# Batch 1 of a cross attention gets the form of batches 2 to 5: two output products in seven blocks, a joint state of y, one subtraction by transfer

## The chip, the cores and the metric

The kernel runs on one core of a Trainium2 chip. The metric is the device time of one execution in microseconds; of several executions the median counts. A core has TensorE (PE, matmuls into PSUM; PEld is its loading of weights), VectorE (DVE), ScalarE (ACT), GpSimd (POOL) and SyncE (SP). Each works through its own queue in order, and the queues meet by semaphores. SP and POOL also start transfers; a transfer that adds to what its destination holds goes out from POOL.

## The reference

Eight batches; x1 and x2 are 512 x 1024 (channels x positions) each, the weights map to 64 channels for queries and keys and to 512 for values, all in float32:

```
q = einsum('bcn,dc->bnd', x1, Wq) + bq
k = einsum('bcn,dc->bdn', x2, Wk) + bk
v = einsum('bcn,dc->bdn', x2, Wv) + bv
attn = softmax(einsum('bnd,bdm->bnm', q, k), axis=2)
out = einsum('bcm,bnm->bcn', v, attn) + x1
```

## The kernel before

The values are never formed. With E the exponentials of the scores (positions of x2 by positions of x1), the kernel computes y = x2 E, scales its columns by one over the sums of E, and then the result Wv y + bv + x1. Both products, y and the result ("o" in names), are 512-row products that are split in 2 x 2 blocks and done in seven block products in place of eight (numbered 1 to 7, `MULT`), with sums of the operands' blocks formed by VectorE beforehand: T1 to T4 of the right operand, S1 to S4 of the left. A block product may be split the same way once more: "in seven blocks" means seven matmul groups of 256 columns in place of plain ones of 512. Its small sums come from `left_stream` and `right_stream` (or `inner_right`), its matmuls from `inner_product` (line 635), or in `multiply_41` from line 1023. Each float32 matmul leaves two records in the trace.

Within a seven-block product the accumulators are shared out with copies on ScalarE: a "chain" in a PSUM bank of its own takes block 1, is copied to one half of a bank, takes block 6, is copied to the next, takes block 5, and so on, so that block 6 can start only when block 1 has been copied. Block 7 (the "third") is copied out to v and added by VectorE at the end: that add is what the calls `complete_7()`, `complete_3()` and so on issue (line 915, in `multiply_41` line 999).

`period(s, n, nn, nnn)` is one batch's stage. It holds the second half of batch s (scaling, products of the result) woven with the first half of batch n, the next one: its scores, the maxima over them (`fold`, `fold_halves`, `highest`), the subtraction of the maximum (`lower`, line 343, 128 x 1024 elements each), and its exponentials. In order, for batch 1: products 1, 2 and 6 of y; scores of the next batch's first half; queries; products 5, 7 and 3 of y; scores of the second half; keys; product 4 of y woven with product 1 of the result (`multiply_41`); products 6, 2, 5, 7, 3 and 4 of the result. Nothing is planned at run time: the schedule is manual, and each engine's queue holds its instructions in the order in which these calls issue them. Hooks (`{6: ...}`) put a ScalarE instruction behind a given block of a product.

Flags of a batch pick between variants. `six` (batches 2 to 6): product 6 of y in seven blocks and y's blocks joined by transfers. `three` (batches 2 to 5): products 3 and 6 of the result in seven blocks, through `ORDER41_3`, which appends product 6 of the result to `multiply_41`, and `multiply_all_573` (5, 7 and 3 together). Batches 0, 1 and 6 do product 6 by `second(6)` (line 521: four plain matmuls of 512 columns) and 5, 7 and 3 by `multiply_57`, where product 3 is plain (line 834).

What the prediction's steps touch:
- `copy_7` (line 1061): ScalarE takes the two halves of product 7 of y, negated, into `tmp[7]`. Half 1 needs `complete_7()`.
- `join_67` (line 1051): VectorE adds `tmp[7]` to `tmp[6]`; `evict_y(s, "22")` (line 1089): VectorE adds that to the accumulator of products 1, 6 and 5 and so forms block 22 of y. In batches 2 to 6 ScalarE copies the accumulator instead (`copy_22`, line 358), and two accumulating transfers add the rest.
- `evict_t3` (line 1066), `scale_y` (line 1073), `sum_y` (lines 478 and 480): blocks of y and their sums.
- `evict_y(s, "21")` and `scale_y(s, "21")`: block 21, which product 2 of the result reads.
- `turn_top` and `lower_late`: the maximum negated on ScalarE, and one of the four subtractions as an accumulating transfer.
- `join_o6`, `copy_o6`: the accumulators of the result's products 1 and 6 joined, and copied out.
- `evict_o`: the result's blocks with bias; block 12 goes through ScalarE without a third summand, or through VectorE with product 3 as one.

Of the kernel before, what the change touches and what calls it, by code (L numbers as in the profile page):

```python
# [11 lines left out]
ALU = mybir.AluOpType  # L12
# [3 lines left out]
def kernel(  # L16
# [47 lines left out]
    nc = tc.nc  # L64
    P = 128
    B, C, N = x1.shape
# [57 lines left out]
    class Batch:  # L124
        def __init__(self, b):
            self.b = b
            self.a, self.e, self.t, self.y, self.o = {}, {}, {}, {}, {}
            self.mx, self.top, self.den, self.few, self.rden, self.row = {}, {}, {}, {}, {}, {}
            self.tmp, self.bank = {}, {}
            self.inner = {}  # L130
            self.six = 2 <= b < B - 1
            self.three = 2 <= b < B - 2
            self.lent = b == B - 2 and not self.six
            self.one = b >= 1

# [19 lines left out]
    def copied_s4(s):  # L155

        s.a["S4"] = sb.tile([P, MH, C // 2], F32, tag="aS4", name=f"aS4_{s.b}")
        nc.scalar.mul(s.a["S4"], s.a["S2"], -1.0)
# [195 lines left out]
    def copy_22(s, j):  # L354

        if j == 0:
            s.y["22"] = sb.tile([P, 2, H], F32, tag="y22", name=f"y22_{s.b}")
        nc.scalar.copy(s.y["22"][:, j, :], s.bank["a", j])
# [45 lines left out]
    def begin_t1(s, i):  # L404
        nc.scalar.mul(s.t["T1"][:, i : i + 2, :], s.t["22"][:, i : i + 2, :], -1.0)
# [147 lines left out]
    def weave(*streams):  # L553

        streams = list(streams)
        while streams:
            for stream in list(streams):
                if next(stream, "end") == "end":
                    streams.remove(stream)
# [32 lines left out]
    def right_stream(s, i, x, *tags):  # L592

        half = x.shape[1] // 2
        v = {f"{q + 1}{r + 1}": x[:, ts(q, half), ts(r, H // 2)] for q in range(2) for r in range(2)}
        last = 4 // len(tags)
        shape = [P, last, half, H // 2]
        sums = [
            sb.tile(shape, F32, tag=t, name=f"eI{i}{t}_{s.b}") if isinstance(t, str) else t for t in tags
        ]  # L600
        if i in (1, 2):
            for z, k in enumerate(("T1", "T2", "T4", "T3")):
                v[k] = sums[z // last][:, z % last]
            s.inner[i, "t"], s.inner[i, "m"] = v, sums[-1][:, last - 2 : last]
            sums_t = (
                ("T1", "12", "11", ALU.subtract),
                ("T3", "22", "12", ALU.add),
                ("T2", "T3", "11", ALU.subtract),
                ("T4", "21", "T2", ALU.subtract),
            )  # L610
            for k, x, y, op in sums_t if i == 1 else sums_t[1:3] + sums_t[:1] + sums_t[3:]:
                nc.vector.tensor_tensor(v[k], v[x], v[y], op)
                yield
            return
        both, t2, t4 = sums[0][:, 0:2], sums[-1][:, last - 2], sums[-1][:, last - 1]
        part = x.rearrange("p (q k) (r n) -> p q k r n", q=2, r=2)
        nc.vector.tensor_tensor(
            both, part[:, :, :, 1, :], part[:, 0].rearrange("p k r n -> p r k n"), ALU.subtract
        )
        s.inner[i, "t"] = v | {"T1": both[:, 0], "T3": both[:, 1], "T2": t2, "T4": t4}  # L620
        yield
        nc.vector.tensor_tensor(t2, both[:, 0], v["22"], ALU.subtract)
        yield
        nc.vector.tensor_tensor(t4, v["21"], t2, ALU.add)
        yield
# [424 lines left out]
    def join_67(s):  # L1050
        nc.vector.tensor_tensor(s.tmp[6], s.tmp[6], s.tmp[7], ALU.add)
# [6 lines left out]
    def copy_7(s, j):  # L1058
        if j == 0:
            s.tmp[7] = sb.tile([P, 2, H], F32, tag="u1", name=f"uy7_{s.b}")  # L1060
        nc.scalar.mul(s.tmp[7][:, j, :], s.bank["c", j], -1.0)
# [253 lines left out]
    def period(s, n, nn, nnn):  # L1315
# [138 lines left out]
            scale_y(s, "11", "T3", "22")  # L1454
        else:
            complete_1 = multiply_seeded(s, 1, "y11", {
                4: lambda: copied_s4(s), 6: lambda: begin_t1(s, 2) if (s.six or s.lent) and s.b > 2 else None
            } if s.b > 1 else {2: lambda: exponential(s, 1, 3)})
            early = s.b > 1 and n is not None
            def second_product():  # L1460
# [94 lines left out]
                for leave in s.leave:  # L1555
                    leave()
            if n:
                sums_3 = right_stream(s, 3, s.t["22"], "eT2" if s.six else "eT1")
                if s.six:
                    if nn is None:  # L1560
                        complete_7()
                    weave(left_stream(s, 3, s.a["S4"], "a12"))
                    if s.b > 1:
                        spread(s, 1)
                    else:
                        shares(s, 1)
                    if nn:
                        complete_7()
                    weave(sums_3)
                else:  # L1570
                    next(sums_3)
                    if s.b == 1:
                        shares(s, 1)
                    weave(*([left_stream(s, 3, s.a["S4"], "aI3")] if nn else []), sums_3)
                if nn or not s.six:
                    lower(n, 0, 0)
            else:
                inner_right(s, 3, s.t["22"], "eT1")
            hooks = {}
            if s.six:  # L1580
                if nn:
                    lower(n, 0, 1)
                complete_5 = multiply_seeded(s, 5, "yT4", {7: lambda: copy_7(s, 0), 6: lambda: copy_7(s, 1)}, "a")
                nc.gpsimd.dma_start(s.tmp[6], s.tmp[7], accum_op=ALU.add)
                complete_5()
                if nn is None:
                    lower(n, 0, 0)
                    lower(n, 0, 1)
                hooks |= {1: lambda: copy_22(s, 0), 7: lambda: copy_22(s, 1)}
            else:  # L1590
                complete_7 = multiply_seeded(
                    s, 7, "y12", {} if n else {6: lambda: copy_22(s, 0), 4: lambda: copy_22(s, 1)}
                )
                complete_7()
                if n is None:
                    shares(s, 1)
                    inner_left(s, 4, s.a["22"], "a12")
                    scale_y(s, "11")
                    inner_right(s, "o1", s.y["11"], "i2")
                copy_7(s, 0)  # L1600
                if n:
                    hooks[7] = lambda: copy_7(s, 1)
                else:
                    copy_7(s, 1)
                    nc.gpsimd.dma_start(s.tmp[6], s.tmp[7], accum_op=ALU.add)
                    nc.gpsimd.dma_start(s.y["22"], s.tmp[6], accum_op=ALU.add)
            if n:
                hooks |= {6: lambda: exponential(n, 0, 0), 4: lambda: exponential(n, 0, 1)}
            if n and not s.six:
                lower(n, 0, 1)  # L1610
            complete_3 = multiply_seeded(s, 3, "r", hooks, "c")
            if s.six:
                if nn:
                    lower(n, 0, 2)
                turn_top(n)
                nc.gpsimd.dma_start(s.y["22"], s.tmp[6], accum_op=ALU.add)
                lower_late(n)
            if n is None:
                right_4 = right_stream(s, 4, s.t["T4"], "eT2")
                next(right_4)  # L1620
            if n and not s.six:
                join_67(s)
                evict_y(s, "22")
            if n is None:
                weave(right_4)
            if n:
                weave(left_stream(s, 4, s.a["22"], "aI3" if s.six else "a12"), right_stream(s, 4, s.t["T4"], "eT1" if s.six else "eT2"))
            if s.six and nn is None:
                complete_3()
                evict_t3(s)  # L1630
            if s.six and s.b > 1:
                scale_y(s, "11")
                inner_right(s, "o1", s.y["11"], "i2")
            if not s.six or nn:
                complete_3()
                evict_t3(s)
        if n:
# [96 lines left out]
        if five:  # L1734
            if nn is None:
                scale_y(s, "22")
            elif not s.three:
                next(sums_o7)
            if s.three:
                products = multiply_all_573(s, while_573)  # L1740
                next(products)
                join_o6(s)
                copy_o6(s)
            sum_y(s, "T1")
            if nn is None:
                next(sums_o7)
                fold(n, 1, 3, "max", ALU.max)
                highest(n, 1)
                weave(sums_o7)
                lower(n, 0, 2, ALU.add)  # L1750
            weave(
                in_turn(lowers(n, 0, MH if s.six else 2, MH), lowers(n, 1, 0, 2)),
                iter(()) if s.three else sums_o7,
            )
        if s.b == 0:
# [16 lines left out]
            second(6)  # L1772
        if s.b == 0:
            exponential(n, 0, 3)
        if five and not s.six:
            exponential(n, 0, 2)
        if s.b == 0:
            negate(n, "S3")
        elif n:
# [146 lines left out]
```

## Time and profile before

| | us |
|---|---|
| median of three runs (lowest, highest) | 660.95 (660.47, 661.91) |
| the profiled execution's own time | 659.96 |
| its span, first to last instruction | 658.2 |
| from batch 1's next scores to batch 2's | 80.34 |
| the same of batches 2, 3, 4, 5 | 79.53, 79.52, 79.70, 79.53 |

In the profile's rows a time is in microseconds from the span's start; a row of a timeline gives start, duration, engine, line, operation, what is written and read, the shape and how many instructions were merged, and in brackets the idle time ahead of it and what ended it. A row of the windows gives the stretch, its length, and each engine's busy time (with the number of its instructions), then TensorE's granted clock, the DMA engines' busy share and what they moved. A TensorE record's end is modelled, so its pace is read from starts. Times of ScalarE, VectorE and TensorE can overlap slightly from one instruction to the next, since they are pipelined.

### The profile page before, as it was taken

What the parts mean: (1) busy time and instruction counts of PE and PEld (TensorE: products, weight loads), DVE (VectorE), ACT (ScalarE), POOL (GpSimd) and SP (SyncE); (2) the same over time, 40 slices, a digit from 0 to 9 for tenths busy, and PEclk for the clock granted to TensorE, in tenths of its full rate; (3) what the DMA queues carried; (4) which work ended last, traced back from release to release, by engine and by line L of the source; (5) the groups of instructions that cost most, each with busy time, mean ns of one, the idle gap of its engine ahead of it and who ended that gap; (6) DMA issues with size and microseconds to landing.
All of it is one profiled execution on the core that took longest, in us unless ns stands there. A gap on an engine that the chain in (4) does not pass through costs nothing.

```text
span 658.2 us, 8303 instructions
## 1 busy us (share of the span) xinstructions
PE 653.7 (99%) x2686; PEld 445.1 (68%) x2686; DVE 623.2 (95%) x907; ACT 409.1 (62%) x804; POOL 233.0 (35%) x208
## 2 busy tenths in 40 slices
PE   9999999999999999999999999999999999999997
PEld 4435755757658667687677786776866777666865
DVE  1999999999899999999999999999999999999996
ACT  3855457446485577865777657776577757575432
POOL 0125215622237322383233822347213553145410
PEclk9999999999999999999999999999999999999999
DMA  9869578994789979999999999999997899789834
GB/s 328 296 218 295 114 252 149 214 259 148 237 177 222 243 232 297 211 199 225 264 308 207 199 253 234 311 209 194 272 262 154 193 195 266 178 161 203 159 81 149
DMA packets 52186, 144.27 MB, mean 219 GB/s; under 512 B 5936, under 2 KB 6448, under 8 KB 52144
## 3 DMA queue, kind: packets, MB, share of 16 engines
q0 software_dynamic: 25152, 70.33, 57.3%
q1 hardware_dynamic: 26848, 73.29, 31.3%
q8 instruction: 21, 0.34, 0.2%
q14 instruction: 21, 0.17, 0.1%
q10 hardware_dynamic: 144, 0.14, 0.1%
HBM read 87.83 MB, written 16.81 MB: 159 GB/s over the span
## 4 chain that ended last, share of the span: by engine, by line
PE 99%; DVE 0%; issue 0%
PE ps_yc L635 9%; PE ps_ya L635 8%; PE ps_oc L521 7%; PE ps_s L238 7%; PE ps_q L193 4%; PE ps_i7chain L635 3%; PE ps_i4b L1023 3%; PE ps_k L193 3%; PE ps_i5chain L635 3%; PE ps_ya L521 3%; PE ps_i3chain L635 3%; PE ps_oa L834 3%; PE ps_oc L1023 3%; PE ps_i1chain L635 3%; PE ps_i2chain L635 3%; PE ps_i4chain L1023 3%
## 5 line engine op out<-in xcount | busy, mean ns | idle before, releaser
L367 ACT ACTIVATE e<-e 128x1024 f32<-128x1024 f32 x60 | 62.9, 1060 | 14.8 <-DVE e L343 14.5
L343 DVE TENSOR_TENSOR e<-e,top 128x1024 f32<-128x1024 f32 x55 | 65.9, 1224 | 0.2 <-POOL top L275 0.2
L275 POOL PARTITION_ALL_REDUCE top<-max x16 | 30.1, 1884 | 81.6 <-DVE max L269 62.4
L247 ACT COPY e<-ps_s 128x512 f32<-128x512 f32 x92 | 48.9, 620 | 11.6 <-PE ps_s L238 9.5
L238 PE MATMUL ps_s<-q,k 64*128 64x512 f32 (+1 forms) x192 | 47.5, 598 | 0.0
L307 POOL PARTITION_ALL_REDUCE den<-sum x10 | 32.6, 3259 | 29.4 <-DVE sum L269 24.5
L259 DVE TENSOR_TENSOR max<-max,e 128x1024 f32<-128x1024 f32 x29 | 35.3, 1218 | 0.6
L238 PEld LDWEIGHTS ps_s<-q,k 64*128 64x128 f32 x192 | 17.9, 186 | 19.9 <-issue 16.0
L1073 DVE TENSOR_TENSOR y<-y,den 128x1024 f32<-128x1024 f32 x24 | 29.2, 1221 | 0.3
L898 ACT COPY ps_yc<-ps_i7chain 128x256 f32<-128x256 f32 x32 | 11.5, 361 | 26.5 <-PE ps_i7chain L635 13.0
L288 POOL PARTITION_ALL_REDUCE den<-sum x6 | 19.4, 3232 | 21.4 <-DVE sum L269 21.4
L193 PE MATMUL ps_q<-x_in_x_dram,wqk_sb 128*64 128x512 f32 x112 | 25.6, 598 | 0.0
L521 PE MATMUL ps_oc<-yT,w 128*128 128x512 f32 x56 | 25.2, 592 | 0.0
L381 DVE TENSOR_TENSOR eT<-e,e 128x1024 f32<-128x1024 f32 (+1 forms) x18 | 24.5, 1384 | 0.1
L898 ACT COPY ps_ya<-ps_i5chain 128x256 f32<-128x256 f32 x32 | 11.4, 357 | 21.2 <-PE ps_i5chain L635 17.0
L586 DVE TENSOR_TENSOR aI<-a 128x256 f32<-128x256 f32 x58 | 23.9, 411 | 0.0
L635 PE MATMUL ps_yc<-e,aI 128*128 128x256 f32 x92 | 23.7, 380 | 0.0
L898 ACT COPY ps_yc<-ps_i3chain 128x256 f32<-128x256 f32 x32 | 11.5, 359 | 16.9 <-PE ps_i3chain L635 12.8
L193 PE MATMUL ps_k<-x_in_x_dram,wqk_sb 128*64 128x512 f32 x96 | 21.9, 598 | 0.0
L328 POOL DMA_DIRECT2D den<-row x12 | 6.7, 555 | 42.9 <-DMA row<-few 37.8
L521 PE MATMUL ps_oc<-y,w 128*128 128x512 f32 x48 | 21.6, 592 | 0.0
L171 POOL DMA_DIRECT2D aS<-in_x2T_dram x7 | 9.8, 1407 | 32.9 <-ACT aS L167 32.9
(431 smaller groups left out, 1961.5 us busy)
## 6 DMA issues: line engine op xcount, KB each, us to landing
x_in_x_dram<-in_x_dram SPq DMA_DIRECT2D x60, 512.0 KB, 9.1
a<-in_x2T_dram SPq DMA_DIRECT2D x32, 512.0 KB, 10.5
eT<-eT POOLq DMA_DIRECT2D x26, 512.0 KB, 8.0
aS<-in_x2T_dram POOLq DMA_DIRECT2D x22, 512.0 KB, 9.1
uo<-in_x_dram POOLq DMA_DIRECT2D x18, 512.0 KB, 11.2
e<-e POOLq DMA_DIRECT2D x14, 512.0 KB, 7.3
out_dram<-uo SPq DMA_DIRECT2D x11, 512.0 KB, 11.9
r<-in_x_dram POOLq DMA_DIRECT2D x10, 512.0 KB, 8.1
```

Of the source, the lines that this page charges most:

```text
L193: nc.tensor.matmul(ps[r, :], w_sb[:, c, :], s.x[:, c, ts(h, H)], start=(c == 0), stop=(c == CT - 1),)
L238: nc.tensor.matmul(ps[g][:, n], s.k[r, ts(i, P)], s.q[r, ts(h, H)][:, n], start=True, stop=True)
L247: nc.scalar.copy(e[:, g, i, :], ps[g])
L259: nc.vector.tensor_tensor(f, e[:, :, 0, :] if i == 1 else f, e[:, :, i, :], op)
L275: nc.gpsimd.partition_all_reduce(s.top[h], s.mx[h][:, 0, :], P, ReduceOp.max)
L307: nc.gpsimd.partition_all_reduce(s.den[h], s.mx[h][:, 0, :], P, ReduceOp.add)
L343: nc.vector.tensor_tensor(e, e, top, op)
L367: nc.scalar.activation(e, e, AF.Exp)
L521: nc.tensor.matmul(ps, left[ka][:, k, ts(j, P)], right[kb][:, k, :], start=opens and k == 0, stop=i in (2, 3, 4) and k == n_k - 1, skip_gr ...
L635: nc.tensor.matmul(ps, s.inner[i][ka][:, k, :], s.inner[i, "t"][kb][:, k, :], start=opens and k == 0, stop=z in (2, 3, 4) and k == n_k - 1 ...
L898: nc.scalar.copy(out, of)
L1023: nc.tensor.matmul(ps, s.inner[i][ka][:, k, :], s.inner[i, "t"][kb][:, k, :], start=opens and k == 0, stop=z in (2, 3, 4) and k == n_k - 1 ...
```

## The change

`three` holds for batch 1 too, so that its result takes the way of batches 2 to 5: product 6 of the result follows product 1 within `multiply_41`, products 5, 7 and 3 come from `multiply_all_573`, block 12 of the result is finished by VectorE, and batch 2's T1 is begun behind a block of its product 1. Beside that, within batch 1: block 22 of y is copied from the accumulator by ScalarE behind blocks 6 and 4 of product 7, both halves of product 7 are copied right behind product 7, and two accumulating transfers form block 22, in place of `join_67` and `evict_y`; of batch 2's four subtractions of the maximum for its first half the third moves ahead of product 4 and the fourth becomes a transfer (`lower_late`); the scaling of block 11 and its sums for product 1 of the result move ahead of `complete_3()`; the third fold of batch 2's second maximum, which batch 1 had left out, is done; the sums for product 3 of y and for product 4 swap their buffers (eT1, eT2).

```
-            self.three = 2 <= b < B - 2
+            self.three = 1 <= b < B - 2
...
-                4: lambda: copied_s4(s), 6: lambda: begin_t1(s, 2) if (s.six or s.lent) and s.b > 2 else None
+                4: lambda: copied_s4(s), 6: lambda: begin_t1(s, 2) if (s.six or s.lent) and s.b > 1 else None
...
-                sums_3 = right_stream(s, 3, s.t["22"], "eT2" if s.six else "eT1")
+                sums_3 = right_stream(s, 3, s.t["22"], "eT2" if s.one and n else "eT1")
...
                 complete_7 = multiply_seeded(
-                    s, 7, "y12", {} if n else {6: lambda: copy_22(s, 0), 4: lambda: copy_22(s, 1)}
+                    s, 7, "y12", {6: lambda: copy_22(s, 0), 4: lambda: copy_22(s, 1)}
                 )
                 complete_7()
...
                 copy_7(s, 0)
-                if n:
-                    hooks[7] = lambda: copy_7(s, 1)
-                else:
-                    copy_7(s, 1)
-                    nc.gpsimd.dma_start(s.tmp[6], s.tmp[7], accum_op=ALU.add)
-                    nc.gpsimd.dma_start(s.y["22"], s.tmp[6], accum_op=ALU.add)
+                copy_7(s, 1)
+                nc.gpsimd.dma_start(s.tmp[6], s.tmp[7], accum_op=ALU.add)
+                nc.gpsimd.dma_start(s.y["22"], s.tmp[6], accum_op=ALU.add)
...
             complete_3 = multiply_seeded(s, 3, "r", hooks, "c")
-            if s.six:
+            if n:
                 if nn:
                     lower(n, 0, 2)
                 turn_top(n)
-                nc.gpsimd.dma_start(s.y["22"], s.tmp[6], accum_op=ALU.add)
+                if s.six:
+                    nc.gpsimd.dma_start(s.y["22"], s.tmp[6], accum_op=ALU.add)
                 lower_late(n)
...
-            if n and not s.six:
-                join_67(s)
-                evict_y(s, "22")
...
-                weave(left_stream(s, 4, s.a["22"], "aI3" if s.six else "a12"), right_stream(s, 4, s.t["T4"], "eT1" if s.six else "eT2"))
+                weave(left_stream(s, 4, s.a["22"], "aI3" if s.six else "a12"), right_stream(s, 4, s.t["T4"], "eT1"))
...
-            if s.six and s.b > 1:
+            if n:
                 scale_y(s, "11")
                 inner_right(s, "o1", s.y["11"], "i2")
-            if not s.six or nn:
+            if n is None or nn:
                 complete_3()
                 evict_t3(s)
...
-                in_turn(lowers(n, 0, MH if s.six else 2, MH), lowers(n, 1, 0, 2)),
+                in_turn(lowers(n, 0, MH, MH), lowers(n, 1, 0, 2)),
                 iter(()) if s.three else sums_o7,
...
-        if five and not s.six:
-            exponential(n, 0, 2)
```

## The prediction

> **What bounds the kernel now.** I read the page first (busy times, then the chain that ended last), then the windows between the first score matmuls of one batch and the next, then each engine's timeline around batch 1 and the same stretch of batch 2, which already has the form that batch 1 is to get.
>
> ```profile
> PE 653.7 (99%) x2686; PEld 445.1 (68%) x2686; DVE 623.2 (95%) x907; ACT 409.1 (62%) x804; POOL 233.0 (35%) x208
> PEclk9999999999999999999999999999999999999999
> PE 99%; DVE 0%; issue 0%
> ```
>
> The chain that ended last is TensorE and nothing else, at the full granted clock. A busy PE row need not mean that its array is always fed, so I look at its pace: the starts of its groups.
>
> ```profile
> core 0: us, PE busy (x) PEld busy (x) DVE busy (x) ACT busy (x) POOL busy (x), PEclk, DMA share, GB/s
> 133.71:214.05 80.34, 80.34 (x330) 55.08 (x329) 77.98 (x115) 50.17 (x96) 29.37 (x24) 1.00 0.84 210
> 155.00:165.00 10.00, 10.00 (x47) 5.70 (x47) 9.96 (x16) 8.56 (x16) 0.54 (x1) 1.00 0.10 30
> 214.05:293.58 79.53, 79.53 (x343) 57.39 (x342) 76.64 (x114) 55.57 (x112) 30.93 (x29) 1.00 0.98 238
> ```
>
> ```profile
> 153.11 1.03 PE L635 MATMUL ps_i3chain<-e,aS 128*128 128x256 f32 x4
> 153.97 1.03 PE L635 MATMUL ps_i3third<-eI3eT,aI 128*128 128x256 f32 x4
> 154.84 1.03 PE L635 MATMUL ps_i3chain<-eI3eT,aI 128*128 128x256 f32 x4
> ...
> 159.25 1.99 PE L238 MATMUL ps_s<-q,k 64*128 64x512 f32 x8
> ...
> 166.47 1.13 PE L1023 MATMUL ps_i4chain<-eT,a 128*128 128x256 f32 x4
> ...
> 175.64 3.60 PE L521 MATMUL ps_oa<-yT,w_S 128*128 128x512 f32 x8
> 179.07 3.60 PE L521 MATMUL ps_oc<-y,w 128*128 128x512 f32 x8
> ...
> 195.82 1.03 PE L635 MATMUL ps_i1chain<-e,a 128*128 128x256 f32 x4
> ```
>
> ```profile
> 246.81 1.13 PE L1023 MATMUL ps_i4chain<-eT,a 128*128 128x256 f32 x4
> ...
> 259.87 3.60 PE L521 MATMUL ps_oc<-y,w 128*128 128x512 f32 x8
> ...
> 275.35 1.03 PE L635 MATMUL ps_i1chain<-e,a 128*128 128x256 f32 x4
> ```
>
> Groups of four 256-column records start 0.86 us apart (153.11, 153.97, 154.84), the eight 512-column records of a plain output product take 3.43 us (175.64 to 179.07), and no gap stands between groups. So TensorE is paced by its own work in both batches: what takes matmul time away shortens the run, and each stall that is added lengthens it for good, since no idle stretch follows in which to catch up. VectorE is the next to bind: 77.98 of the 80.34 us from batch 1's scores to batch 2's, and 76.64 of the following 79.53.
>
> **The change part by part.** *TensorE's saving.* Products 3 and 6 of the result go from 8 records of 512 columns to 14 of 256 each: 14 x 0.86/4 = 3.02 us in place of 3.43, 0.41 each, 0.82 in all. The two batches say the same: from product 4 of y to the next batch's first product, batch 1 takes 195.82 - 166.47 = 29.35 us and batch 2 275.35 - 246.81 = 28.54. Saving: 0.81 us.
>
> *ScalarE's order.* Block 22 of y now comes from the accumulator by two copies while product 7 runs, and both copies of product 7 stand ahead of product 3, where the second stood behind product 3's second block.
>
> ```profile
> 153.31 0.60 ACT L1061 ACTIVATE uy<-ps_yc 128x512 f32<-128x512 f32 x1 [0.51 <-PE ps_yc L635]
> 154.23 0.36 ACT L898 COPY ps_yc<-ps_i3chain 128x256 f32<-128x256 f32 x1 [0.32 <-PE ps_i3chain L635]
> ...
> 155.31 0.60 ACT L1061 ACTIVATE uy<-ps_yc 128x512 f32<-128x512 f32 x1
> ```
>
> ```profile
> 149.10 1.69 DVE L617 TENSOR_TENSOR eI3eT<-e 128x1024 f32<-128x1024 f32 x1
> ...
> 154.46 0.69 DVE L915 TENSOR_TENSOR ps_yc<-ps_yc,v 128x512 f32<-128x512 f32 x1
> 155.06 1.21 DVE L343 TENSOR_TENSOR e<-e,top 128x1024 f32<-128x1024 f32 x1
> 156.19 1.21 DVE L1051 TENSOR_TENSOR uy<-uy,uy 128x1024 f32<-128x1024 f32 x1
> 157.44 1.29 DVE L1089 TENSOR_TENSOR y<-ps_ya,uy 128x512 f32<-128x512 f32 x2
> 158.65 0.41 DVE L586 TENSOR_TENSOR aI<-a 128x256 f32<-128x256 f32 x1
> ...
> 162.32 0.69 DVE L915 TENSOR_TENSOR ps_yc<-ps_yc,v 128x512 f32<-128x512 f32 x1
> ...
> 173.20 0.70 DVE L999 TENSOR_TENSOR ps_oc<-ps_oc,v 128x512 f32<-128x512 f32 x1 [0.79 <-ACT ps_oc L1032]
> ...
> 175.48 0.70 DVE L999 TENSOR_TENSOR ps_i4b<-ps_i4b,v 128x512 f32<-128x512 f32 x1 [0.99 <-ACT ps_i4b L1032]
> ...
> 177.53 1.23 DVE L1073 TENSOR_TENSOR y<-y,den 128x1024 f32<-128x1024 f32 x1
> ```
>
> The second copy of product 7 reads what VectorE's add at 154.46 leaves at 155.15; nothing ahead of that add moves in VectorE's queue. Handing over costs 0.09 us (product 3's first group ends at 153.11 + 1.03, ScalarE starts at 154.23). So that copy runs from 155.24 to 155.84, and behind it in ScalarE's queue waits the copy of product 3's chain (0.36), which stood at 154.23 and now ends at 156.2. TensorE's third block of product 3 adds to that chain and must wait for it: 156.3 in place of 154.84, a stall of 1.4 us. Its bounds: 0 if the add came before 153.9, 1.4 as the rows stand. The two copies of block 22 (0.6 each, the copy at 153.31 being as large) fall into the waits that ScalarE has during product 7 and cost nothing.
>
> *VectorE ahead of product 4.* The sum of products 6 and 7 and the two sums into block 22 (156.19 to 158.65, 2.46 us) go. In their place comes the third subtraction of the maximum (1.13, as from 155.06 to 156.19), so the sums for product 4 begin at 157.32. They take 3.67 (158.65 to 162.32) and end at 160.99. Then, ahead of the add that completes product 3, come the scaling of block 11 and the sums for the result's product 1, which stood behind it. Batch 2 has that order:
>
> ```profile
> 238.60 1.22 DVE L1073 TENSOR_TENSOR y<-y,den 128x1024 f32<-128x1024 f32 x1
> ...
> 241.39 0.69 DVE L915 TENSOR_TENSOR ps_yc<-ps_yc,v 128x512 f32<-128x512 f32 x1
> ...
> 252.22 1.22 DVE L1073 TENSOR_TENSOR y<-y,den 128x1024 f32<-128x1024 f32 x1
> 253.55 0.70 DVE L999 TENSOR_TENSOR ps_oc<-ps_oc,v 128x512 f32<-128x512 f32 x1
> ...
> 258.19 1.22 DVE L1073 TENSOR_TENSOR y<-y,den 128x1024 f32<-128x1024 f32 x1
> ```
>
> These are 2.79 us (238.60 to 241.39): product 3 is completed at 163.78 in place of 162.32.
>
> *VectorE from there to block 21.* Next come, as in batch 2, a third fold of the maximum (batch 1 left it out), the sums for the result's products 6, 7 and 3, the adds of product 4, and block 21 with its scaling: 258.19 + 1.22 - 241.39 = 18.02 us in batch 2. Of these 0.2 is a wait: 252.22 to 253.55 is 1.33, where an operation of that size moves the queue on by 1.13. Late as it is, batch 1 does not meet this wait, so 17.8: block 21 is scaled at 181.6. Now it is scaled at 178.76, after two idle stretches (0.79, 0.99) that the new work fills.
>
> *Who waits for it.* The result's product 2 reads block 21. By batch 2's pace TensorE reaches it at 166.47 + (259.87 - 246.81) = 179.53; with handing over it starts at 181.7. So TensorE ends up 2.17 us behind batch 2's pace. The stall of 1.4 in product 3 is part of that and not on top of it: VectorE's queue waits for nothing that the first stall delays (product 3 then ends at 159.25 + 1.4, VectorE needs it at 163.78), so the larger of the two counts. Behind product 2 nothing more is lost, as the rest follows at the pace that batch 2 shows.
>
> *Transfers.* GpSimd's queue gets two accumulations of 512 KB in series, then the maximum's, ahead of the one for S1.
>
> ```profile
> 156.76 0.54 POOL L328 DMA_DIRECT2D den<-row  x1 [5.04 <-PE ps_i3chain L635]
> ```
>
> ```profile
> DMA to landing us min/median/max: 4.7/9.9/10.2
> ```
>
> This queue stands until 156.76 for a row, so the first goes out at 157.3. Block 22 is needed at 163.78 + (252.22 - 241.39) = 174.6. The second row tells the landings of the same transfers in batch 2: with 4.7 each and 0.5 between them block 22 is there at 167.2, with 10.2 each at 178.2. I take the short ones, since the DMA engines are at 0.10 between 155 and 165 us, and charge nothing. The maximum's transfer takes one subtraction (1.13) from VectorE; the count above has it left out already.
>
> **Sum.** +2.17 - 0.81 = +1.36 us. Against the profiled execution's 659.96: 661.3. That one lies 0.99 below the median of the runs shown; the forecast for a median is 660.95 + 1.36 = 662.3. Uncertain in it: VectorE operations that meet a reduction of GpSimd run longer (1.69 at 149.10, where 1.21 is usual), up to +0.5 for one more such meeting and +1.0 for two; waits hidden in batch 2's 18.02, down to -0.5. The forecast's own range is 661.8 to 663.3.
>
> **The rivals.**
> *VectorE keeps up, and the saving stays* (not slower). If batch 2's 18.02 us are stretched by TensorE's pace, which VectorE follows there, a late queue runs through them faster. It decides at 179.53: the chain would have to be done 2.1 us earlier, and the first stall would have to vanish with an earlier add at 154.46. Then 660.95 - 0.81 = 660.1. Against it: starts in these rows follow each other by the operations' own durations, and I find 0.2 us. Chance 0.13.
> *Only the copy stalls*: VectorE keeps up, the add does not come earlier: 1.4 - 0.81 = +0.6, 661.5. Chance 0.05.
> *Block 22 lands late*: at 178.2 it holds VectorE for 3.6 us more, 665.9. It decides at 174.6. For it, 9.9 is the median of batch 2's landings; against it, those ran with DMA engines at 0.98, these with 0.10. Chance 0.06.
> *The clock falls behind the stalls.* If TensorE's clock were halved after its idle stretches, as at the start, it would lose half of such a stretch:
>
> ```profile
> L1231 PE MATMUL ps_warm<-warm 128*128 128x128 f32 x14 | 3.4, 432 | 1.0 <-DVE warm L1228 1.0
> ```
>
> These first 14 records of 128 columns take 3.4 us, 0.24 each, where the pace of 0.86/4 for 256 columns makes 0.11. A stretch of that length at half rate costs 1.7 more, 664.0. Two stalls of 1.4 and 0.8 us are small beside it, and the clock row shows nothing under 9. Chance 0.03. The Trainium skill (TensorE: Matmul & The Clock Gate, Part 1: The HAM clock gate) has the clock at half rate again after an idle window of about 3.4 us; by that rule these stalls are too short, and no row of this kernel shows an idle stretch of such a length after the start.
> *TensorE has room.* Its weight loads are busy 68% of the span, its matmuls 99%; if the 68% told its load, neither saving nor stall would show: 660.95. The starts 0.86 us apart speak against it. Chance 0.03. The Trainium skill (Perfetto Trace Analysis, Identifying the Most-Contended Engine) calls matmul busy time a poor measure and weight-load time a better one; here the pace of the starts decides, and it sides with the matmuls.
>
> **How the numbers follow.** What is left, 0.70, is the forecast: 662.3. A measurement of this kernel tells apart about 0.2%, 1.3 us (its three runs go from 660.47 to 661.91). The forecast lies at that bound; its uncertainty leans upward, so 0.42 of its 0.70 are slower by more and 0.28 within. Slower: 0.42 + 0.06 + 0.03 = 0.51. Faster by over 0.2% could only come from the first rival with a lucky median, 0.03. The rest is within: 0.46. The range goes from the first rival to the forecast's upper end, 660.0 to 663.5; late landing, a fallen clock and the forecast's tail stay outside, under 0.2.
>
> **What would show it.** Right: TensorE's third block of product 3 in batch 1 about 1.4 us behind its second; ScalarE's second copy of product 7 ahead of product 3's first; VectorE without idle time from 154 to 181 us; the result's product 2 starting right behind block 21's scaling at about 181.7; batch 2's scores 1.4 us later than 214.05. Wrong: product 2 at 179.5 with no gap (then VectorE had reserves), or a gap ahead of the scaling of block 22 (then transfers rule).

## The result, and the profile after

| | before | after |
|---|---|---|
| median (lowest to highest), 17 runs each | 660.74 (659.84 to 661.91) | 662.64 (661.54 to 666.91) |
| ratio, with its 95% interval | 1 | 1.0034 (1.0021 to 1.0047) |
| profiled execution, its span | 659.96, 658.2 | 662.27, 660.5 |

The changed kernel is slower by 1.9 us. A later measurement of both gave 662.29 (661.23 to 663.15, 11 runs) beside 660.66 (23 runs): 1.0020 (1.0011 to 1.0028), 1.6 us.

The page of the changed kernel: the busy times, the clock row and the chain that ended last.

```profile
PE 654.2 (99%) x2698; PEld 446.7 (68%) x2698; DVE 627.1 (95%) x915; ACT 414.2 (63%) x817; POOL 235.5 (36%) x211
PEclk9999999999999999999999999999999999999999
PE 94%; DVE 5%; issue 1%; ACT 0%; DVEq 0%
```

The busy shares tell nothing of the change. The chain does: VectorE, with 0% of it before, now holds 5% of the span. TensorE's waits in the profile say where (engine and line, whom it waited for, us in total, times, longest):

```profile
PE ps_i3chain L635 <- ACT ps_yc L898: 1.3, 1, 1.3
...
PE ps_oc L521 <- DVE y L1073: 0.3, 1, 0.3
```

Both are new and lie in batch 1. From here on I call **the stretch** the time from TensorE's first group of batch 1's product 3 to its first group of batch 2's product 1, and compare kernels by it. Its windows, first of the kernel before, then of the changed one (columns as in the prediction's windows):

```profile
153.11:195.82 42.71, 42.71 (x157) 26.01 (x156) 40.72 (x59) 31.00 (x54) 9.21 (x9) 1.00 0.64 169
```

```profile
153.92:198.22 44.30, 42.69 (x169) 28.04 (x168) 43.37 (x65) 33.26 (x65) 11.16 (x12) 1.00 0.84 208
```

The stretch is 1.59 us longer. TensorE stands for 1.61 of it (44.30 - 42.69), VectorE is busy for all but 0.93, the clock stays at 1.00. Of the 2.31 us between the two profiled executions, 1.59 are here, and 0.81 lie ahead of the stretch (153.92 - 153.11). I take that second part for scatter: two profiles of one kernel (the "lighter" one below) reached this point at 153.82 and 153.02. From the stretch's end on the kernels differ by 0.1 us.

TensorE's timeline in the stretch, after:

```profile
153.92 1.03 PE L635 MATMUL ps_i3chain<-e,aS 128*128 128x256 f32 x4
154.78 1.03 PE L635 MATMUL ps_i3third<-eI3eT,aI 128*128 128x256 f32 x4
157.08 1.13 PE L635 MATMUL ps_i3chain<-eI3eT,aI 128*128 128x256 f32 x4 [1.27 <-ACT ps_yc L898]
158.05 1.03 PE L635 MATMUL ps_yc<-e,aS 128*128 128x256 f32 x4
...
180.14 0.59 PE L1023 MATMUL ps_io6chain<-eIo,w_IS 128*128 128x256 f32 x2
180.78 0.70 PE L635 MATMUL ps_io3chain<-y,w_S 128*128 128x256 f32 x2
181.32 0.59 PE L635 MATMUL ps_io6third<-eIo,w_IS 128*128 128x256 f32 x2
181.75 0.59 PE L635 MATMUL ps_oa<-yT,w_IS 128*128 128x256 f32 x2
182.64 3.70 PE L521 MATMUL ps_oc<-y,w 128*128 128x512 f32 x8 [0.29 <-DVE y L1073]
186.18 0.59 PE L635 MATMUL ps_io7chain<-yT,w 128*128 128x256 f32 x2
...
198.22 1.03 PE L635 MATMUL ps_i1chain<-e,a 128*128 128x256 f32 x4
```

A bracket counts from the modelled end of the record before, so what a wait costs is read from starts. The third block of product 3 starts 2.30 us after the second where 0.86 is the pace: 1.44 lost. The chain of the result's product 3 starts 0.64 behind a pair that takes 0.43: 0.21 lost, with no bracket at all. The result's product 2 starts 0.89 behind such a pair: 0.46 lost. And the first group after each of the three waits takes 0.11 longer to the next start (0.97 for 0.86, 0.54 for 0.43, 3.54 for 3.43): 0.33. Together 2.44. Without them the stretch would be 41.86, which is 0.85 under the 42.71 of before: the saving is there, and the waits cost more.

VectorE and ScalarE in the same stretch, after:

```profile
155.44 0.69 DVE L915 TENSOR_TENSOR ps_yc<-ps_yc,v 128x512 f32<-128x512 f32 x1
...
164.76 0.69 DVE L915 TENSOR_TENSOR ps_yc<-ps_yc,v 128x512 f32<-128x512 f32 x1
...
170.09 2.55 DVE L259 TENSOR_TENSOR max<-max,e 128x1024 f32<-128x1024 f32 x2
...
175.59 1.22 DVE L1073 TENSOR_TENSOR y<-y,den 128x1024 f32<-128x1024 f32 x1
...
180.05 1.27 DVE L1087 TENSOR_TENSOR y<-uy,ps_i4b 128x512 f32<-128x512 f32 x2
181.36 1.22 DVE L1073 TENSOR_TENSOR y<-y,den 128x1024 f32<-128x1024 f32 x1
```

```profile
154.12 0.60 ACT L1061 ACTIVATE uy<-ps_yc 128x512 f32<-128x512 f32 x1
156.16 0.60 ACT L1061 ACTIVATE uy<-ps_yc 128x512 f32<-128x512 f32 x1 [1.44 <-DVE ps_yc L915]
156.65 0.38 ACT L898 COPY ps_yc<-ps_i3chain 128x256 f32<-128x256 f32 x1
```

On ScalarE the second copy of product 7 (L1061) waits 1.44 us for VectorE's add, and the copy of product 3's chain stands behind it until 156.65; TensorE's block follows at 157.08. On VectorE no row from 154 to 181 us has a bracket any more, neither those shown nor those between; in before, the adds at 173.20 and 175.48 had 0.79 and 0.99 us of idle time ahead of them. Block 21 is evicted at 180.05 (L1087), which gives free the accumulator that the 180.78 group needs, and scaled by 182.58, and product 2 starts 0.06 later. Batch 2's first scores start at 216.45, which is 1.59 later than the 214.05 of before when the later start of 0.81 is taken off; the prediction had 1.4.

### The profile page after: what moved, and what is told of

The parts are those of the page before. It is cut to its first block, busy times and chain, and to the rows that moved or that the text cites. A ratio compares the mean times of both kernels' runs of the same rounds, so it can differ in the third digit from the quotient of the medians.

```text
span 660.5 us, 8355 instructions
## 1 busy us (share of the span) xinstructions
PE 654.2 (99%) x2698; PEld 446.7 (68%) x2698; DVE 627.1 (95%) x915; ACT 414.2 (63%) x817; POOL 235.5 (36%) x211
## 4 chain that ended last, share of the span: by engine, by line
PE 94%; DVE 5%; issue 1%; ACT 0%; DVEq 0%
PE ps_yc L635 9%; PE ps_ya L635 8%; PE ps_oc L521 7%; PE ps_s L238 6%; PE ps_q L193 4%; PE ps_i5chain L635 3%; PE ps_ya L521 3%; PE ps_i7chain L635 3%; PE ps_i4b L1023 3%; PE ps_i3chain L635 3%; PE ps_i1chain L635 3%; PE ps_i2chain L635 3%; PE ps_k L193 3%; PE ps_oa L802 3%; PE ps_oc L1023 2%; PE ps_i4chain L1023 2%
## 5 line engine op out<-in xcount | busy, mean ns | idle before, releaser
L417 POOL DMA_DIRECT2D e<-e x14 | 13.9, 1008 | 16.8 <-ACT e L367 14.4
```

## The experiments

**1. Is it chance where the stretch begins?** The kernel before once more, and later the changed kernel and the lighter one of experiment 6 once more; no edit.

> The kernel before, profiled a second time. In the first profile TensorE reaches batch 1's product 3 at 153.1 us, in the changed kernel at 153.9, though nothing ahead of it was changed. If that is chance of the first microseconds (waits for the first loads), this profile has another value, near 153.9, and the same stretch from product 3 to batch 2's product 1, 42.7 us. If the change moved it by way of addresses or code, it is 153.1 again.

Measured: 660.22, stretch 42.71 (153.25 to 195.97), the same to 0.01 us. By itself its start, 153.25, is nearer to 153.1 than to 153.9 and does not settle the question.

> The changed kernel, profiled and timed again beside the lighter version. Theory A: stretch 44.3 again (it hangs on the order of the queues and not on chance), time 1.6 to 1.9 us over before. What ahead of batch 1 differs (152.1 to 153.3 us so far) is chance of the first loads and varies again.

Measured: stretch 44.46 (154.72 to 199.18), the block of product 3 with a bracket of 1.44, product 2 with 0.29; median and ratio stand above. The stretch repeats to 0.2 us, its start does not: 153.92 and 154.72 for the changed kernel, 153.82 and 153.02 for the lighter one, 153.0 to 154.7 over all profiles (the expectation's "152.1 to 153.3" is about 1 us too low). So the start is scatter, and what follows compares stretches first and medians second. The runs of up to 666.9 in the first measurement did not come back; nothing here shows their cause.

**2. The copy goes back behind product 3's second block; all else as changed.** My theory, A, is that VectorE's lateness at block 21 sets the loss, with the copy's stall hidden inside it. The rival, B, is that the new order of the copies is the loss by itself.

```
 copy_7(s, 0)
-copy_7(s, 1)
-nc.gpsimd.dma_start(s.tmp[6], s.tmp[7], accum_op=ALU.add)
-nc.gpsimd.dma_start(s.y["22"], s.tmp[6], accum_op=ALU.add)
+if n:
+    hooks[7] = lambda: copy_7(s, 1)
...
 complete_3 = multiply_seeded(s, 3, "r", hooks, "c")
+if n and not s.six:
+    nc.gpsimd.dma_start(s.tmp[6], s.tmp[7], accum_op=ALU.add)
+    nc.gpsimd.dma_start(s.y["22"], s.tmp[6], accum_op=ALU.add)
```

> The changed kernel with one thing undone: ScalarE's second copy of product 7 stands behind block 7 of product 3 again, as before. Measure: the stretch on TensorE from batch 1's product 3 to batch 2's product 1 (42.71 us before, 44.30 after). Theory A (VectorE's late block 21 sets the loss, the copy's stall of 1.44 us lies inside it): the stall in product 3 goes, the ones at block 21 grow by as much, product 2 of the result still starts 0.06 us behind the scaling of block 21; stretch 44.3, time unchanged within 0.2 us of the changed kernel. Theory B (the order of the copies sets the loss): stretch 42.9, time 1.4 us shorter than the changed kernel.

Measured: 662.46 (661.78 to 662.66) beside 660.83, ratio 1.0025 (1.0014 to 1.0035); stretch 44.44. TensorE's timeline in this kernel:

```profile
153.91 1.03 PE L635 MATMUL ps_i3chain<-e,aS 128*128 128x256 f32 x4
...
180.91 0.70 PE L635 MATMUL ps_io3chain<-y,w_S 128*128 128x256 f32 x2 [1.28 <-DVE y L1087]
...
182.77 3.70 PE L521 MATMUL ps_oc<-y,w 128*128 128x512 f32 x8 [0.30 <-DVE y L1073]
```

The stall in product 3 is gone and the time is not: 1.28 us now stand at 180.91, where the result's product 3 waits for block 21's eviction, and product 2 starts 28.86 us into the stretch (28.72 in the changed kernel). B falls. The two stalls do not add; the later one is what the earlier one leaves of VectorE's lateness.

**3. One more operation on VectorE.** The third fold is done twice in batch 1.

```
+if s.b == 1:
+    fold(n, 1, 3, "max", ALU.max)
```

> The changed kernel with the third fold of the maximum done twice in batch 1, which leaves its result as it is: one more VectorE operation of 1.13 us ahead of block 21. Theory A: product 2 of the result starts 1.13 us later, stretch 45.4, time +1.1 us over the changed kernel. Theory B, in which VectorE has reserve there: stretch 44.3, no change.

Measured: 662.86 (662.73 to 663.99), ratio 1.0038 (1.0023 to 1.0053); stretch 45.69. TensorE's timeline in this kernel:

```profile
157.61 1.13 PE L635 MATMUL ps_i3chain<-eI3eT,aI 128*128 128x256 f32 x4 [1.41 <-ACT ps_yc L898]
...
182.56 0.70 PE L635 MATMUL ps_io3chain<-y,w_S 128*128 128x256 f32 x2 [1.28 <-DVE y L1087]
...
184.42 3.70 PE L521 MATMUL ps_oc<-y,w 128*128 128x512 f32 x8 [0.29 <-DVE y L1073]
```

The stall in product 3 stays as it was, and the stretch is 1.23 to 1.39 longer than in the changed kernel's two profiles. The expectation counted 1.13 for the fold. In VectorE's merged rows two folds take 2.55 in the changed kernel (170.09) and three take 3.81 in this one, which makes one 1.26; so its time reaches the end in full.

**4. One operation less.** Batch 1 leaves the third fold out, as it did before. (The maximum that is subtracted then leaves out one tile of four.)

```
-fold(n, 1, 3, "max", ALU.max)
+if s.b > 1:
+    fold(n, 1, 3, "max", ALU.max)
```

> The changed kernel without the third fold of batch 2's second maximum (as before the change; the maximum that is subtracted then leaves out one tile of four). VectorE is 1.13 us earlier at block 21, the copy's stall of 1.44 stays. Theory A: block 21 is ready at about the time at which TensorE, held only by the copy, comes for it: the gain stops at 0.8 us, stretch 43.5. Theory B: the copy's stall alone counts, the fold is hidden: stretch 44.3, no change.

Measured: 661.44 (660.71 to 663.93), ratio 1.0017 (1.0007 to 1.0027); stretch 43.49. TensorE's timeline in this kernel:

```profile
157.12 1.13 PE L635 MATMUL ps_i3chain<-eI3eT,aI 128*128 128x256 f32 x4 [1.33 <-ACT ps_yc L898]
...
181.91 3.60 PE L521 MATMUL ps_oc<-y,w 128*128 128x512 f32 x8
```

Product 2 no longer waits. Only 0.81 of the fold comes back: below that the copy's stall, which has stayed, is the larger of the two. This is the other side of experiment 2: the loss is the maximum of two stalls, not their sum.

**5. The parts taken apart.** First the joint state of y alone (copies, transfers, fourth subtraction), with products 3 and 6 of the result in eight blocks as before.

```
-self.three = 1 <= b < B - 2
+self.three = 2 <= b < B - 2
...
-    begin_t1(s, 2) if (s.six or s.lent) and s.b > 1 else None
+    begin_t1(s, 2) if (s.six or s.lent) and s.b > 2 else None
...
 elif five:
-    scale_y(s, "11")
-    weave(right_stream(s, "o1", s.y["11"], "i2"), in_turn(singly(lambda: scale_y(s, "T3")), folds(n, 1, "max", ALU.max, 2)))
+    scale_y(s, "T3")
+    fold(n, 1, 1, "max", ALU.max)
...
+if five and not s.six:
+    exponential(n, 0, 2)
```

> Only the joint state of y, its copies, the transfers and the moved scaling; products 3 and 6 of the result plain as before. VectorE has less to do than before and is in time at block 21. Theory A: the copy's stall (1.44 us and 0.1 for the restart) stands alone and counts in full, stretch 44.2, time 1.5 us over before. If the copy's stall were made up by later slack, stretch 42.7.

Measured: 662.13 (661.57 to 664.23) beside 660.61, ratio 1.0027 (1.0016 to 1.0038); stretch 44.09. TensorE's timeline in this kernel:

```profile
156.51 1.13 PE L635 MATMUL ps_i3chain<-eI3eT,aI 128*128 128x256 f32 x4 [1.11 <-ACT ps_yc L898]
...
180.84 3.60 PE L521 MATMUL ps_oc<-y,w 128*128 128x512 f32 x8
```

Without the third fold and the sums for seven blocks VectorE is not late, product 2 waits for nothing, and the copy's stall stands alone: 42.71 to 44.09 is 1.38, where start to start it is 1.28 and 0.11 for the first group after it. So a stall that was worth nothing in the changed kernel (experiment 2) is worth all of itself here.

Then the changed kernel without the joint state: block 22 summed on VectorE and the second copy where it was before. The seven blocks stay, and with them the third fold, the moved scaling and the fourth subtraction by transfer.

```
-s, 7, "y12", {6: lambda: copy_22(s, 0), 4: lambda: copy_22(s, 1)}
+s, 7, "y12", {} if n else {6: lambda: copy_22(s, 0), 4: lambda: copy_22(s, 1)}
...
-copy_7(s, 1)
+if n:
+    hooks[7] = lambda: copy_7(s, 1)
+else:
+    copy_7(s, 1)
...
+if n and not s.six:
+    join_67(s)
+    evict_y(s, "22")
```

> The changed kernel with the joint state undone: products 6 and 7 joined and block 22 formed by VectorE (2.46 us as in the profile of before), the copies of product 7 in the order of before; the rest as changed. Theory A: no copy stall, but VectorE 2.4 us later at block 21: product 2 of the result starts 2.4 us later, stretch 46.7, time 2.4 us over the changed kernel. Theory B (the copies' order sets the loss): stretch 42.0, time 2.3 under the changed kernel.

Measured: 665.06 (664.01 to 665.70), ratio 1.0073 (1.0056 to 1.0089); stretch 46.60. TensorE's waits in this kernel:

```profile
PE ps_oa L1023 <- ACT ps_oa L1032: 1.4, 1, 1.4
PE ps_io3chain L635 <- DVE y L1087: 1.3, 1, 1.3
...
PE ps_oc L1023 <- DVE yT L1066: 0.7, 1, 0.7
PE ps_oc L521 <- DVE y L1073: 0.3, 1, 0.3
```

The sums into block 22 are back in VectorE's queue, everything behind them is later, and TensorE waits at four places. So the joint state is what makes the seven blocks bearable in batch 1, and it does not take enough from VectorE to make them pay.

**6. A lighter version.** Experiments 2 and 4 together, but with the two transfers into block 22 apart (the first behind product 3, the second behind the maximum's third), and batch 2's third subtraction of the maximum as one more `lower_late`. If A holds, the saving should be all that is left. (As in 4, the maximum leaves out one tile.)

```
-def lower_late(s):
+def lower_late(s, i=3):
...
-    nc.gpsimd.dma_start(s.e[0][:, :, 3, :], top, accum_op=ALU.add)
+    nc.gpsimd.dma_start(s.e[0][:, :, i, :], top, accum_op=ALU.add)
...
 complete_3 = multiply_seeded(s, 3, "r", hooks, "c")
+if n and not s.six:
+    nc.gpsimd.dma_start(s.tmp[6], s.tmp[7], accum_op=ALU.add)
...
-if nn:
+if nn and s.six:
     lower(n, 0, 2)
 turn_top(n)
-if s.six:
-    nc.gpsimd.dma_start(s.y["22"], s.tmp[6], accum_op=ALU.add)
+if not s.six:
+    lower_late(n, 2)
+nc.gpsimd.dma_start(s.y["22"], s.tmp[6], accum_op=ALU.add)
 lower_late(n)
```

> The changed kernel with the copy behind block 7 of product 3, without the third fold, and with the third subtraction of the maximum by transfer as well (ahead of the second accumulation for block 22): no copy stall, and VectorE 2.26 us earlier at block 21. Theory A: TensorE waits nowhere in the stretch by more than 0.2 us; stretch 41.9 to 42.2, time 2.1 to 2.4 us shorter than the changed kernel and 0.5 to 0.8 shorter than before. Theory B: stretch 42.9, as with the copy alone. If the transfer lands behind the time at which ScalarE's exponential wants it (about 172 us), ScalarE holds product 4 up and the stretch is longer than 42.5.

Measured: 660.82 (659.59 to 663.41) beside 660.83, ratio 1.0006 (0.9993 to 1.0019); stretch 41.97.

> The lighter version again. Stretch 42.0 again. Whether VectorE waits for block 22 in batch 2 (1.1 us the first time) depends on when that transfer lands, within a margin of 1 to 3 us either way: if it waits again, the rest of the run is 459.4 us and the time before's; if not, 458.4 and 0.7 under before.

Measured: 660.55 (659.03 to 662.16, 12 runs) beside 660.66, ratio 0.9996 (0.9987 to 1.0006); stretch 41.89. The windows of this second one, the stretch and what follows it until batch 2's end, then VectorE, then TensorE in batch 2:

```profile
153.02:194.91 41.89, 41.89 (x169) 28.31 (x168) 40.91 (x62) 33.10 (x65) 12.44 (x13) 1.00 0.93 232
194.91:276.88 81.97, 80.06 (x342) 57.18 (x340) 78.14 (x116) 55.73 (x113) 31.94 (x31) 1.00 1.00 234
```

```profile
253.90 1.23 DVE L1073 TENSOR_TENSOR y<-y,den 128x1024 f32<-128x1024 f32 x1 [1.91 <-DMA y<-uy]
```

```profile
259.09 0.70 PE L635 MATMUL ps_io3chain<-y,w_S 128*128 128x256 f32 x2 [1.27 <-DVE y L1087]
261.29 3.70 PE L521 MATMUL ps_oc<-y,w 128*128 128x512 f32 x8 [0.64 <-DVE y L1073]
```

In batch 1 it does what A says: TensorE stands for nothing (41.89 of 41.89), and the stretch is 0.82 shorter than before, which is the saving. In batch 2 it is lost again in both profiles, now by a transfer: block 22 lands 1.91 us after VectorE wants it (1.10 in the first profile), and TensorE waits at the same two places as in batch 1 of experiment 2. From batch 2's product 1 to batch 3's it then takes 81.97 us (80.42 in the first profile) where the kernel before takes 79.53, so that 2.44 and 0.89 are lost against a saving of 0.82. From batch 2's product 1 to the span's end there are 462.4 us in before, 463.2 and 465.1 here. So no version beats the kernel before by what can be measured. Why block 22 lands late the rows tell only in part. GpSimd's timeline in batch 2, first before, then the changed kernel, in which VectorE does not wait for block 22, then the lighter one:

```profile
199.79 3.23 POOL L288 PARTITION_ALL_REDUCE den<-sum  x1 [2.69 <-DVE sum L269]
...
244.87 0.88 POOL L1616 DMA_DIRECT2D y<-uy  x1 [9.86 <-ACT e L247]
```

```profile
203.81 3.23 POOL L288 PARTITION_ALL_REDUCE den<-sum  x1 [3.58 <-DVE sum L269]
...
248.00 0.87 POOL L1614 DMA_DIRECT2D y<-uy  x1 [9.28 <-DMA uy<-uy]
```

```profile
200.50 3.23 POOL L288 PARTITION_ALL_REDUCE den<-sum  x1 [3.58 <-DVE sum L269]
...
245.70 0.88 POOL L1621 DMA_DIRECT2D y<-uy  x1 [9.35 <-DMA uy<-uy]
```

Behind batch 2's product 1 (195.82, 198.22 and 194.91) the reduction that VectorE's sum releases comes 3.97, 5.59 and 5.59 us later. Those 1.6 us are VectorE's, whose sum (L285) starts 1.92 us behind product 1 in before and 3.54 in the other two. But they do not explain the late landing, as the changed kernel has them too and does not wait. The second of the two transfers into block 22 goes out 49.05, 49.78 and 50.79 us behind product 1 and takes 4.7, 5.4 and 8.2 us to land (7.3 in the first profile of the lighter kernel). So of the 5.2 us by which block 22 lands later than in before, 3.5 are the landing itself. What makes it long is not shown, and no run tries this by itself.

**7. The divisors' row on SyncE's queue.** GpSimd issues that transfer ahead of block 22's, so I moved it, in the lighter kernel and in the changed one.

```
-queue = nc.sync if s.b >= B - 2 else nc.gpsimd
+queue = nc.sync if s.b >= B - 2 or h == 1 and s.b else nc.gpsimd
```

> The lighter version (copy behind block 7, no third fold in batch 1, two of the four subtractions by transfer) with the broadcast of the second half's divisors issued by SyncE in place of GpSimd in batches 1 to 5, so that GpSimd's queue does not stand for the row ahead of block 22's transfers. In the lighter version batch 2's block 22 landed at 253.56 us and VectorE waited 1.1 us for it, which TensorE lost again. Theory C (what the lighter version gains in batch 1 it loses in batch 2 by late landings): in batch 2 the first of block 22's transfers goes out 2 to 3 us earlier, VectorE waits for none, the stretch stays at 42.0, the rest of the run from batch 2's product 1 is 458.4 us as in the kernel before; time 0.6 to 0.8 us under before. If the landing depends on the DMA engines' load alone, it stays at about 253 and the time at before's.

Measured: 663.40 (662.51 to 665.48) beside 660.90, ratio 1.0034 (1.0021 to 1.0048); stretch 41.98.

> The changed kernel with the same move of the divisors' broadcast to SyncE. The loss in batch 1 does not hang on it: Theory A gives stretch 44.3 and a time 1.6 us over before. The runs of the changed kernel reached from 661.5 to 666.9 us, those of before from 659.8 to 661.9; if single late landings of block 22 make that tail, no run lies more than 2 us over the median here.

Measured: 665.87 (665.30 to 667.53), ratio 1.0081 (1.0067 to 1.0095); stretch 44.26. Both missed: the time behind the stretch grew. VectorE's waits from 200 to 600 us, of the first and of the second:

```profile
DVE yT L1073 <- DMA den<-row: 6.6, 4, 2.5
```

```profile
DVE yT L1073 <- DMA den<-row: 5.6, 4, 2.0
```

On SyncE's queue the row itself lands late in batches 2 to 5 (246.06 in batch 2 of the lighter kernel, 242.65 in its first profile without the move), and VectorE waits for it instead; in batch 2 it no longer waits for block 22. From batch 2's product 1 to the span's end there are 467.5 and 466.2 us. The first transfer into block 22 went out 39.0 us behind product 1 where the lighter kernel's two profiles have 40.2 and 40.5, a gain of 1.2 to 1.5 in place of the 2 to 3 that were expected; the profile names nothing that it waited for. So these runs leave open whether a batch 2 with an early block 22 would keep the saving.

**8. Sums handed to GpSimd.** In batch 1 the sums of weights for the result's products 3 and 6 (L659, of 128x128) leave VectorE for GpSimd; `left_values` takes the engine as an argument.

```
-weave(left_values("o3", "S4"), left_values("o6", "S2"))
+weave(left_values("o3", "S4", nc.gpsimd), left_values("o6", "S2", nc.gpsimd))
```

> The changed kernel with the eight small sums of the value weights for products 3 and 6 of the result (3.7 us of VectorE's queue at 138 to 142 us) computed on GpSimd. VectorE is then up to 3.7 us earlier from there on. Theory A: the add of product 7 comes in time for the copy, and block 21 in time for product 2: no stall over 0.2 us, stretch 41.9 to 42.2, time 2.2 us under the changed kernel and 0.6 to 0.8 under before, if block 22 of batch 2 lands in time. Theory B, with the loss in the products' order itself: stretch 44.3. GpSimd's own queue gets longer by the eight operations; if that holds up the reduction for the next maximum, VectorE waits there, and the stretch is between.

Measured: 675.49 (674.36 to 676.37), ratio 1.0226 (1.0211 to 1.0242); stretch 56.67. It missed altogether. GpSimd's timeline in this kernel, and then the windows within TensorE's stall and behind it:

```profile
154.27 0.86 POOL L659 TENSOR_TENSOR w_IS<-w_S 128x128 f32<-128x128 f32 x2 [9.82 <-issue]
...
163.49 1.80 POOL L275 PARTITION_ALL_REDUCE top<-max  x1 [5.89 <-issue]
```

```profile
158.00:158.50 0.50, 0.00 (x0) 0.00 (x0) 0.00 (x0) 0.00 (x0) 0.00 (x0) 1.00 0.00 0
158.50:159.00 0.50, 0.00 (x0) 0.00 (x0) 0.00 (x0) 0.00 (x0) 0.00 (x0) 0.55 0.00 0
...
168.00:172.00 4.00, 3.88 (x9) 3.18 (x10) 4.00 (x7) 1.78 (x4) 1.48 (x2) 0.50 0.28 54
172.00:176.00 4.00, 4.00 (x18) 2.66 (x19) 3.90 (x8) 2.41 (x5) 0.00 (x0) 0.97 0.74 152
```

The eight sums themselves take 3.4 us. Ahead of them GpSimd stands 9.8 us and behind them 5.9, "issue" in both, so the profile names no one it waited for; then comes the reduction of the maximum, for which VectorE, ScalarE and at last TensorE wait (12.5 us at product 3's third block). As an attempt to relieve VectorE the run is void; what it shows of the chip stands in the last section.

## Why the prediction was right

**TensorE's saving, 0.81.** Right: 0.85 from the changed kernel's starts with its waits taken out, 0.82 from the lighter kernel's stretch.

**The copy's stall, 1.4.** Right: 1.44 from start to start, by the steps foreseen (the second copy of product 7 behind VectorE's add, the chain's copy behind it in ScalarE's queue). Left out was that the first group after a wait takes another 0.11 us.

**VectorE to block 21.** Right: from the add to the end of block 21's scaling the prediction counted 27.1 us (154.46 to 181.6), and 27.14 were measured (155.44 to 182.58). From the completion of product 3 it counted 17.8 and the rows give 17.82 (164.76 to 182.58), so batch 2's queue did tell batch 1's. With the stretch's later start taken off (0.81), product 2 started at 181.83 where 181.7 was forecast.

**The larger stall counts, not the sum.** Right, and the one step that the rows of before could not show. Experiments 2 to 5 show it from both sides: taking away the earlier stall moved the wait to block 21 and did not shorten the time, and taking work from VectorE helped by 0.81 and then stopped at the earlier stall.

**Transfers cost nothing.** Right for batch 1: block 22 landed at 169.0 and was read at 175.59, 6.6 us to spare where the prediction had 7.4. The two landings took 5.9 and 4.6 us where the prediction counted 4.7 each. Its reason for the short ones was that the DMA engines were at 0.10. That is not shown: the 4.7 itself is from batch 2, where the engines were at 0.75 while that transfer ran. The lighter kernel shows how little of that cover batch 2 has.

**The sum, +1.36.** The stretch gave +1.59. The 0.23 are small terms: product 2 started 2.33 us behind its pace (2.44 less the slower first group behind it) where 2.17 were counted, as VectorE's add came 1.52 us behind product 3's first group and not 1.35; that slower group adds 0.11; and the saving was 0.85 and not 0.81. One of those waits was not foreseen: block 21's eviction also holds the accumulator that the result's product 3 needs (0.21 at 180.78). It lies within VectorE's lateness and so took nothing on top.

That the median came as near as 662.64 to the forecast of 662.3 is in part luck. The change was forecast at +1.36 and measured at +1.90, 0.54 more; but the 660.95 that it was added to, a median of three runs, was 0.21 above the 660.74 of 17 runs, and that hid part of the difference. Of the 0.54, 0.23 are in the stretch; the other 0.31 are not explained. The later measurement, +1.63 beside a stretch of +1.75, has no such rest.

**The rivals.** VectorE did not keep up, since the waits are there; the copy's stall alone is what experiment 5 made and the changed kernel is not; TensorE has no room, as each stall of 1.3 to 1.4 us appears in the stretch; block 22 did not land late in batch 1. The clock did not fall: 1.00 in the stretch, with stalls of up to 1.4 us. That rival's mechanism is real, though. In experiment 8 TensorE stands from 155.6 on, the modelled end of its last record; the granted clock is 1.00 until 158.5 and 0.55 on average over the next half microsecond, 0.50 after that. So it fell some 3.0 us into the idle time, and a stall of 1.4 us is too short for it. The Trainium skill (TensorE: Matmul & The Clock Gate, Part 1: The HAM clock gate) has the half rate follow an idle window of about 3.4 us; this trace agrees to within 0.4 us. At 0.50 groups of four started 1.86 and 1.71 us apart where 0.86 is usual. The prediction took the slow records at the start (0.24 us each) for half rate too; the profile of before does not show that, since its granted clock is 1.00 over the first 5 us.

## What to carry to other kernels

When one engine is busy 99% of a stretch and the next 97%, add up the second one's queue through that stretch before taking 0.8 us from the first: here the saving came in full, and the work that bought it made VectorE the one that sets the time. Two stalls in a row on one engine count as the larger of them when the source of the second does not wait for the first, so taking one away alone can change nothing, and a stall that is free in one version costs all of itself in another. And what is gained in one batch can be lost in the next, here to a transfer that landed late for a reason left open, so look one batch further before calling a gain a gain.

## What the runs showed of the hardware

- The first TensorE group after a wait of 0.2 to 1.4 us takes 0.11 us longer to the next start (0.97 for 0.86, 3.54 for 3.43), at a granted clock of 1.00. In an idle time of 12.5 us the clock fell to 0.50 after about 3.0 us (experiment 8, at 158.5); it stayed there until 172.2, 4.1 us after TensorE had started again at 168.12, and was 1.00 from then on.
- VectorE's first sum for product 3 of y (L617, 128x1024 elements) took 1.69 us in before (149.10) and in the changed kernel (150.07), where GpSimd's reduction over partitions started 0.4 us ahead of it (148.68 and 149.65) and ran beside it; in experiment 8, where that reduction came only at 163.49, the same sum took 1.21.
- GpSimd stood 9.8 us between an all-reduce over partitions with its transfers and its first elementwise sum, and 5.9 us between the last sum and the next all-reduce, for 3.4 us of sums. The profile names no releaser for either gap. One kernel, one profile; whether it is the change of operation was not tried apart.
